# Ones beside the values in the first self-attention, and two preparations moved in program order

## The chip, the cores and the metric

The kernel runs on one core of one Trainium2 chip. The metric is the device time of one execution in microseconds (us). Engines are named PE (TensorE, matrix multiplication), DVE (VectorE), ACT (ScalarE), POOL (GpSimd) and SP (SyncE, which here only issues transfers). Line numbers such as L463 are those of the kernel before.

## The reference

The program is a small two-layer decoder over x of 4 x 256 x 256, with a context ctx_2048 of 4 x 1601 x 256 and a padding mask of 4 x 1601. For the change only the first layer matters: a self attention with 16 heads of 16, then an attention over the context with the mask, then a feed forward whose two weights are made ternary. Cut to the steps concerned:

```python
w = softmax(where(causal, q @ k.T / sqrt(16), -inf))    # 16 heads of 16, per batch
x = x + (w @ v) @ Wo + bo
s = where(mask, NEG, layernorm(x) @ ctx.T)              # 1601 context rows, per batch
x = x + softmax(s) @ ctx
gamma = mean(abs(w))                                    # for w_fc and w_proj, once
w_hat = sign(round(w / (gamma + 1e-6))) * gamma         # ternary weight
```

## The kernel before

The four batches (b = 0 to 3) pass one after another, and overlapping, through four generators: self_attention (L336), memory_attention (L524), feed_forward (L633) and recurrence (L694). A loop of ticks (from L1372) advances each generator by one step per tick; batch b starts at tick START[b] = 0, 3, 9, 15. From some point on a second part takes over, with an attention over the context by pairs of heads and experts, which fills most of the span; the change does not touch it.

The order of instructions on each engine is not written out by hand. The generators emit a program, and a scheduler decides each engine's queue from it. There is one means to hold it: `behind` (L1349) advances a generator and ties every instruction it emits after the latest instruction emitted so far on the same engine. It is used for the first two steps of batches 1 to 3, for the making of the ternary weights and for the first tables of the second part.

self_attention, per batch: layer norm, transposition to features, projection to queries and keys (pq, added to the bias on DVE at L371) and values (pv, L377, added at L381 into a tile v of the batch, 256 values per row), rotation, and norms per head. Then four groups of four heads (c = 0, 1 and e = 0, 1; the names carry batch, c, e, so sc2110 is batch 2, c = 1, e = 1, first half). For each group:

- scores sc: a causal mask is put into the banks with bf16 matmuls (L445), then query times key (L451). Two double banks exist, and one group uses both.
- row maxima mx on DVE (L455, L456), then eight exponentials on ACT (L463), each of which also accumulates its row sum in `sums`;
- the reciprocal of the sums on DVE (L467);
- transposes of the probabilities on PE (tpp L474, tpq L480), copied to SBUF: pT by ACT (L475), tpq's by DVE (L483);
- attention times values on PE (po, L489 and L492), with 32 columns of values at a time, that is two heads of which one is used; copied by ACT (oT, L496), transposed back (tb, L500), and multiplied with the reciprocals on DVE into `a` (L502).

At the end `a` is transposed, multiplied with wo and added to x (L516, L520).

memory_attention, per batch: its first step prepares the mask. A tile mk of bytes is set to zero by DVE, two small transfers on SP's queue fill it, DVE makes from it a float mask mf (L533) and a count cnt (L535), PE transposes mf and sums cnt (xpm, L537 and L538), and DVE copies the results (mb, ok, from L540). mk, mf and cnt have one buffer each. Then come a norm, scores against the transposed context in four pieces (xcT, 512 KB each on SP's queue, xsc L562) with mb as the bias (L565), maxima (xacc, L569 to L573; xtm, xbc), exponentials, and the product with the context (xct, xpo L607). Pieces of the context, and the temporaries `neg` of shared_weights, share the NDB = 3 buffers of one tag.

shared_weights (L303), called tern in the loop: per weight (wfc, wpj: 128 x 2048 each) a sum of magnitudes on DVE (L309), a matmul that adds over partitions (pgg, L311), small operations for the thresholds, then twice a comparison (L323) and a multiplication-like step (L324) of 128 x 1024; at the end a small table hmr (16 KB) is loaded on ACT's queue and two tiles of kron are made. It begins at tick TERN = 20 and goes one step per tick.

Of the kernel before, what the change touches and what calls it, by code (L numbers as in the profile page):

```python
# [20 lines left out]
P = 128  # L21
B, S, D = 4, 256, 256
# [3 lines left out]
NKEY = S + S2  # L26
NCH = 15
NS = 12
H0, HD0 = 16, 16
NKV, REP, HD1 = 4, 4, 128  # L30
# [1 line left out]
NA = 3  # L32
NDB = 3
NROPE = 3
TERN = 20
SIDE = 24
SIDEN = 4
RATE = 1
# [71 lines left out]
def decoder_kernel(ctx: ExitStack, tc: tile.TileContext, at, t, out):  # L110
    nc = tc.nc
    V, A, G, T = nc.vector, nc.scalar, nc.gpsimd, nc.tensor
# [41 lines left out]
    def fa(b, name, dt=F32):  # L154

        return fr.tile([P, 512], dt, tag=f"a{b}", name=name, bufs=NA)
# [9 lines left out]
    def sm(shape, tag, name, bufs=2, dt=F32):  # L166
        return small.tile(shape, dt, tag=tag, name=name, bufs=bufs)

    xs = [const.tile([P, 2, D], F32, tag=f"x{b}", name=f"x{b}") for b in range(B)]

    def load_x(b):
# [47 lines left out]
    def moments(xb, nm):  # L221

        mv = sm([P, 2, 2], "mv", f"mv_{nm}")
        for j in range(2):
            st = sm([P, 6], "bnst", f"st_{nm}{j}")
            V.bn_stats(st, xb[:, j, :])
            V.bn_aggr(mv[:, j, :], st)
        return mv

    def rsqrt(v, eps, nm, n=2):  # L230

# [55 lines left out]
    bqkv, bo, dtb = rows[:, 0:768], rows[:, 768:1024], rows[:, 1024:1280]  # L287
# [48 lines left out]
    def self_attention(b):  # L336
# [25 lines left out]
        for j in range(2):  # L362
            js = slice(j * P, (j + 1) * P)
            pq = p1(f"pq{b}{j}")
            for e in range(2):
                for c in range(2):
                    T.matmul(
                        pq[:, e * 256 : e * 256 + 256], lhsT=xx[:, e, c, js], rhs=wqkv[:, c, e * 256 : e * 256 + 256],
                        start=c == 0, stop=c == 1,
                    )  # L370
            V.tensor_add(qk[:, j, :], pq, bqkv[:, 0:512])  # L371
            yield
        v = fa(b, f"v{b}").rearrange("p (j d) -> p j d", j=2)
        pv = p1(f"pv{b}")
        for j in range(2):
            for c in range(2):
                T.matmul(  # L377
                    pv[:, j * 256 : j * 256 + 256], lhsT=xx[:, 1, c, j * P : (j + 1) * P], rhs=wqkv[:, c, 512:768],
                    start=c == 0, stop=c == 1,
                )  # L380
        V.tensor_add(v, pv.rearrange("p (j d) -> p j d", j=2), bqkv[:, None, 512:768].to_broadcast([P, 2, D]))  # L381

        hd = [P, 2, 32, HD0]
        q4 = qk.rearrange("p j (h d) -> p j h d", d=HD0)
# [4 lines left out]
        rs = cc("r0s").rearrange("p (j d two) -> p j d two", j=2, two=2)  # L389
# [27 lines left out]
        yield  # L417

        if b == 0:
            for e in range(2):  # L420
                V.tensor_scalar(
                    qln[:, e, :], cols[:, 20:22], 1.0 / math.sqrt(HD0), cc("par")[:, e : e + 1], ALU.mult, ALU.mult
                )
        tq = to_features(qkn[:, :, 0:256], f"q{b}")
        qm = fb(b, f"qm{b}").rearrange("p (e n) -> p e n", e=2)
        V.tensor_scalar(qm[:, 0, :], tq, qln[:, 0, 0:1], qln[:, 0, 1:2], ALU.mult, ALU.add)
# [2 lines left out]
        kT = fa(b, f"kT{b}")  # L429
# [4 lines left out]
        for c in range(2):  # L434
            for e in range(2):


                nm = f"{b}{c}{e}"
                mx = sm([P, 2, 4], "mx4", f"mx{nm}", 4)
                sums = sm([P, 2, 4], "sums", f"sum{nm}", 4)  # L440
                scs, es = [], []
                for u in range(2):
                    sc = p2(f"sc{nm}{u}")[0].rearrange("p (h k) -> p h k", h=2)
                    for h in range(2):
                        T.matmul(sc[:, h, 0:384], lhsT=identb, rhs=trib.rearrange("p i k -> p (i k)"), start=True, stop=False)  # L445
                    scs.append(sc)
                q0 = c * 256
                for lo, hi, k0, k1, n in ((0, P, 0, P, P), (P, 2 * P, P, 3 * P, 2 * P)):
                    for i in range(4):
                        r = slice(32 * i, 32 * (i + 1))  # L450
                        T.matmul(  # L451
                            scs[i // 2][:, i % 2, k0:k1], lhsT=qm[r, e, q0 + lo : q0 + hi], rhs=kT[r, c, 0:n], start=False, stop=lo > 0
                        )
                for u in range(2):
                    V.tensor_reduce(mx[:, 0, 2 * u : 2 * u + 2], scs[u][:, :, 0:128], AX.X, ALU.max, negate=True)  # L455
                    V.tensor_reduce(mx[:, 1, 2 * u : 2 * u + 2], scs[u][:, :, 128:384], AX.X, ALU.max, negate=True)  # L456
                yield
                for u in range(2):
                    ex = fb(b, f"sm{nm}{u}").rearrange("p (h k) -> p h k", h=2)
                    for h in range(2):  # L460
                        for j, k in enumerate((slice(0, 128), slice(128, 384))):
                            i = 2 * u + h
                            A.activation(  # L463
                                ex[:, h, k], scs[u][:, h, k], AF.Exp, bias=mx[:, j, i : i + 1], accum_out=sums[:, j, i : i + 1]
                            )
                    es.append(ex)
                V.reciprocal(sums.rearrange("p j h -> p (j h)"), sums.rearrange("p j h -> p (j h)"))  # L467
                yield
                pT = fb(b, f"pT{nm}").rearrange("p (h t) -> p h t", h=4)
                for u in range(2):  # L470
                    tp = p1(f"tpp{nm}{u}")
                    for h in range(2):
                        for j in range(2):
                            T.transpose(tp[:, (2 * h + j) * P : (2 * h + j + 1) * P], es[u][:, h, j * P : (j + 1) * P], ident)  # L474
                    A.copy(pT[:, 2 * u : 2 * u + 2, :].rearrange("p h t -> p (h t)"), tp)  # L475

                tp = p1(f"tpq{nm}")
                for u in range(2):
                    for h in range(2):
                        T.transpose(tp[:, (2 * u + h) * P : (2 * u + h + 1) * P], es[u][:, h, 256:384], ident)  # L480
                for u in range(2):
                    src = tp[:, 2 * u * P : 2 * (u + 1) * P].rearrange("p (h t) -> p h t", h=2)
                    V.tensor_copy(es[u][:, :, 384:512], src)  # L483
                yield

                po = p1(f"po{nm}")
                for i in range(4):
                    f = slice(c * P + 32 * i, c * P + 32 * i + 32)
                    T.matmul(po[32 * i : 32 * i + 32, 0:256], lhsT=v[:, 0, f], rhs=pT[:, i, :], start=True, stop=False)  # L489
                for i in range(4):  # L490
                    f = slice(c * P + 32 * i, c * P + 32 * i + 32)
                    T.matmul(  # L492
                        po[32 * i : 32 * i + 32, 128:256], lhsT=v[:, 1, f], rhs=es[i // 2][:, i % 2, 384:512], start=False, stop=True
                    )
                oT = es[0][:, 0, 0:256]
                A.copy(oT, po[:, 0:256])  # L496
                yield
                tb = p1(f"tb{nm}")
                for j in range(2):
                    T.transpose(tb[:, j * P : (j + 1) * P], oT[:, j * P : (j + 1) * P], ident)  # L500
                for j in range(2):
                    V.tensor_mul(  # L502
                        a[:, j, c * P : (c + 1) * P].rearrange("p (r e d) -> p r e d", e=2, d=16)[:, :, e, :],
                        tb[:, j * P : (j + 1) * P].rearrange("p (r e d) -> p r e d", e=2, d=16)[:, :, e, :],
                        sums[:, j, :, None].to_broadcast([P, 4, 16]),
                    )
                yield
        G.tensor_tensor(xb, xb, bo[:, None, :].to_broadcast([P, 2, D]), ALU.add)
# [15 lines left out]
    def memory_attention(b):  # L524
        xb = xs[b]
        last = S2 - 12 * P

        mk = sm([NC2, P], "mk", f"mk{b}", 1, U8)
        V.memset(mk, 0.0)
        nc.sync.dma_start(out=mk[0:12, :], in_=t["mask"][b, 0 : 12 * P].rearrange("(c p) -> c p", p=P))  # L530
# [9 lines left out]
        V.tensor_copy(mb, pm[:, 0:NC2])  # L540
        ok = sm([P, 1], "ok", f"ok{b}")
        V.tensor_scalar(ok, pm[:, 64:65], 1.0, None, ALU.min)
        mv = moments(xb, f"xa{b}")
        r1 = rsqrt(mv[:, :, 1], 1e-5, f"xa{b}")
        yield
# [7 lines left out]
        for i in range(4):  # L553
            n = 4 if i < 3 else 1
# [793 lines left out]

    def behind(gen, end=None):  # L1349

        ins = nc.cur_bb.bb.instructions
        n = len(ins)
        said = next(gen, end)
        latest = {}
        for i in ins[:n]:
            latest[i.engine] = i
        for i in ins[n:]:
            if i.engine in ENGINES and i.engine in latest:
                tc.add_manual_dep(
                    i, latest[i.engine].name,  # L1360
                    mybir.DependencyInfo(mybir.DependencyClass.NoSync, mybir.DependencyReason.DATA), reason="order",
                )
        return said


# [102 lines left out]
```

## Time and profile before

| what | us |
|---|---|
| median of 3 runs | 1842.06 (1841.42 to 1842.9) |
| the profiled execution | 1839.59 |
| its span | 1837.7, granted clock 0.971 |
| PE busy | 1727.6 (94%) |
| DVE busy | 1288.4 (70%) |
| ACT busy | 1007.2 (55%) |
| POOL busy | 871.8 (47%) |

The profile is of one execution. A group's row has engine, operation and tile, count, busy time, mean duration in ns and the idle time just before its instructions; a row of the timeline has start, duration and, in brackets, the idle time before and what ended it. Granted clock is the share of full speed that PE's throttle allowed. The page's picture of the span in 40 slices of 46 us, cut to four rows, shows PE less busy in the first three or four slices than later:

```profile
PE   4779899989999999999999999999999999999997
DVE  5785647787777677777767786776768676766754
ACT  1556536464656555675656566565746465555631
...
PEclk8789899999999999999999999999999999999998
```

In the chain that ended last, PE has 72% of the span, DVE 10%, ACT 8% and POOL 6%; the largest lines of the chain belong to the second part.

### The profile page before, as it was taken

The numbers are of one execution on the slowest core, as the hardware profiler recorded it, in microseconds if no ns is written. First come the engines' busy times: TensorE is split into PE (matmuls) and PEld (weight loads), VectorE is DVE, ScalarE is ACT, GpSimd is POOL, SyncE is SP. The second block draws the span as 40 slices with busy tenths as digits, with TensorE's granted clock in tenths as the row PEclk, the third lists the DMA queues.
The fourth block names the chain that finished last, engine by engine and source line by source line (L and its number), as shares of the span: only waits on it lengthen the run. The fifth ranks groups of instructions, "written<-read, shape, count | busy, mean of one in ns | idle before, by whom it ended". The sixth has DMA issues, their size and how long they took to land.

```text
span 1837.7 us, 20229 instructions
## 1 busy us (share of the span) xinstructions
PE 1727.6 (94%) x6576; PEld 1051.1 (57%) x6576; DVE 1288.4 (70%) x2396; ACT 1007.2 (55%) x1896; POOL 871.8 (47%) x716
## 2 busy tenths in 40 slices
PE   4779899989999999999999999999999999999997
PEld 3456786655555554645555555656565655656555
DVE  5785647787777677777767786776768676766754
ACT  1556536464656555675656566565746465555631
POOL 2100232111277566566656465555647574555560
PEclk8789899999999999999999999999999999999998
DMA  4010231100210110102010111201111211111110
GB/s 139 1 39 17 73 119 61 32 24 25 67 55 15 52 34 33 38 30 65 17 62 27 63 35 49 61 29 55 34 62 33 68 38 52 32 35 44 32 38 23
DMA packets 66216, 83.00 MB, mean 45 GB/s; under 512 B 6460, under 2 KB 49600, under 8 KB 66112
## 3 DMA queue, kind: packets, MB, share of 16 engines
q1 hardware_dynamic: 64960, 80.31, 14.1%
q10 hardware_dynamic: 1152, 1.41, 0.2%
q8 instruction: 53, 0.87, 0.2%
q14 instruction: 51, 0.42, 0.1%
HBM read 80.65 MB, written 1.05 MB: 44 GB/s over the span
## 4 chain that ended last, share of the span: by engine, by line
PE 72%; DVE 10%; ACT 8%; POOL 6%; issue 4%; POOLq 0%; DVEq 0%; ACTq 0%
PE bsc L1181 18%; PE bpo L1221 17%; PE pk L1115 11%; POOL sum L1212 3%; PE bpw L1247 3%; PE mph L914 2%; PE xpo L607 2%; ACT s L1206 2%; PE xsc L562 2%; ACT s L1182 2%; PE pq L1078 2%; PE mpe L925 1%; ACT sm L463 1%; PE pp L689 1%; PE tpk L1124 1%
## 5 line engine op out<-in xcount | busy, mean ns | idle before, releaser
L1212 POOL TENSOR_TENSOR sum<-sum,s 128x512 f32<-128x512 f32 (+1 forms) x416 | 541.0, 1301 | 81.9 <-ACT s L1206 55.5
L1181 PE MATMUL bsc<-qTb,kTb 128*128 128x512 f32 (+1 forms) x960 | 457.9, 597 | 3.3 <-ACT kTb L1126 3.3
L1221 PE MATMUL bpo<-s,vb 128*128 128x512 f32 (+1 forms) x960 | 456.0, 593 | 0.0
L1182 ACT ACTIVATE s<-bsc,kn 128x512 f32<-128x512 f32 (+1 forms) x480 | 317.8, 685 | 186.1 <-PE bsc L1181 164.4
L1186 DVE SCALAR_TENSOR_TENSOR acc<-bsc,kn,acc 128x512 f32<-128x512 f32 x448 | 333.6, 745 | 110.0 <-ACT s L1182 100.4
L1203 DVE TENSOR_TENSOR s<-s,bc 128x1024 f32<-128x1024 f32 (+1 forms) x256 | 288.4, 1141 | 14.2 <-PE bc L1199 14.0
L1206 ACT ACTIVATE s<-s 128x1024 f32<-128x1024 f32 (+1 forms) x256 | 256.1, 1009 | 60.7 <-DVE s L1203 59.9
L1181 PEld LDWEIGHTS bsc<-qTb,kTb 128*128 128x128 f32 (+1 forms) x960 | 172.1, 187 | 187.8 <-issue 145.8
L1221 PEld LDWEIGHTS bpo<-s,vb 128*128 128x128 f32 (+1 forms) x960 | 173.4, 191 | 141.3 <-issue 136.6
L1040 POOL TENSOR_TENSOR ropek<-ropek,ropuk 128x512 f32<-128x512 f32 (+1 forms) x64 | 76.9, 1201 | 255.9 <-DVE ropuk L1035 255.9
L1115 PE MATMUL pk<-wkv,cTk 128*128 128x256 f32 x832 | 190.1, 379 | 0.0
L1115 PEld LDWEIGHTS pk<-wkv,cTk 128*128 128x128 f32 x832 | 156.7, 190 | 28.4 <-issue 6.2
L1209 POOL TENSOR_TENSOR sum<-s 128x512 f32<-128x512 f32 x32 | 41.8, 1306 | 186.7 <-ACT s L1206 186.7
L1034 DVE TENSOR_TENSOR ropek<-pk,ctabk 128x256 f32<-128x256 f32 (+1 forms) x128 | 51.8, 404 | 70.6 <-ACT squares L1033 69.9
L1033 ACT ACTIVATE squares<-pk 128x256 f32<-128x256 f32 (+1 forms) x128 | 48.1, 377 | 96.3 <-PE pk L1115 74.7
L1047 ACT ACTIVATE ropeq<-ropeq,rnq 128x128 f32<-128x128 f32 x128 | 41.9, 390 | 107.4 <-POOL rnq L1043 107.4
L1184 DVE TENSOR_SCALAR acc<-bsc,kn 128x512 f32<-128x512 f32 x32 | 24.0, 749 | 83.5 <-ACT s L1182 83.5
L1118 ACT COPY vb<-pk 128x256 f32<-128x256 f32 (+1 forms) x128 | 46.3, 362 | 58.7 <-DVE ropuk L1035 56.0
L463 ACT ACTIVATE sm<-sc,mx 128x128 f32<-128x128 f32 (+1 forms) x128 | 52.2, 435 | 26.5 <-DVE mx L456 19.6
L1043 POOL TENSOR_TENSOR kn<-ssk,nhalf 128x4 f32<-128x4 f32 (+1 forms) x64 | 65.5, 1024 | 0.0
L914 PE MATMUL mph<-yTm,wi 128*128 128x256 f32 x256 | 63.2, 392 | 0.0
L1040 POOL TENSOR_TENSOR ropeq<-ropeq,ropuq 128x512 f32<-128x512 f32 x32 | 41.1, 1284 | 40.5 <-DVE ropuq L1035 40.5
(491 smaller groups left out, 2482.8 us busy)
## 6 DMA issues: line engine op xcount, KB each, us to landing
cTk<-in_ctxT SPq DMA_DIRECT2D x32, 512.0 KB, 3.6
wq<-in_wq SPq DMA_DIRECT2D x16, 512.0 KB, 4.9
wo<-in_wo SPq DMA_DIRECT2D x16, 512.0 KB, 4.0
wi<-in_wi SPq DMA_DIRECT2D x32, 256.0 KB, 2.9
xcT<-in_ctxT SPq DMA_DIRECT2D x12, 512.0 KB, 3.7
xct<-in_ctx SPq DMA_DIRECT2D x12, 512.0 KB, 3.7
cTk<-in_ctxT SPq DMA_DIRECT2D x16, 384.0 KB, 3.2
wkv<-in_wkv SPq DMA_DIRECT2D x16, 256.0 KB, 3.8
```

The lines of the kernel that those rows point to most:

```text
L463: A.activation(ex[:, h, k], scs[u][:, h, k], AF.Exp, bias=mx[:, j, i : i + 1], accum_out=sums[:, j, i : i + 1])
L914: T.matmul(ph[:, i * 256 : i * 256 + 256], lhsT=wi[:, i, c, f * ME : (f + 1) * ME], rhs=yT[:, c, :], start=c == 0, stop=c == 1,)
L1040: G.tensor_tensor(r4, r4, u4[:, :, ::-1, :], ALU.add)
L1043: G.tensor_tensor(rn, ss[:, 0:n], nhalf[:, 0:n], ALU.pow)
L1115: T.matmul(pk[:, q, :], lhsT=src, rhs=e["wkv"][:, c, :], start=c == 0, stop=c == 1)
L1181: T.matmul(pc[0:n, :], lhsT=e["kT"][:, k * P : k * P + n], rhs=q, start=True, stop=True)
L1182: A.activation(s[0:n, i, :], pc[0:n, :], AF.Copy, scale=e["kn"][0:n, k : k + 1])
L1186: V.scalar_tensor_tensor(self.acc[0:n, :], pc[0:n, :], e["kn"][0:n, k : k + 1], self.acc[0:n, :], ALU.mult, ALU.max)
L1203: V.tensor_tensor(s[0:n, 0:w, :], s[0:n, 0:w, :], self.bc[0:n, None, :].to_broadcast([n, w, 512]), ALU.subtract)
L1206: A.activation(s[0:n, 0:w, :], s[0:n, 0:w, :], AF.Exp)
L1212: G.tensor_tensor(self.sum[0:n, :], self.sum[0:n, :], s[0:n, i, :], ALU.add)
L1221: T.matmul(self.po, lhsT=e["v"][0:n, k, :], rhs=self.s[c][0:n, i, :], start=k == 0, stop=k == NCH - 1)
```

## The change

Five edits. (1) The values move from a tile of each batch to eight tiles `spots` that lie in buffers otherwise used only later; each head has 32 columns, 16 values and 16 ones, and the ones are set once by POOL at the start. The matmul po then takes the 32 columns of one head, and its columns 16 to 31 give the row sums. The exponentials no longer accumulate sums; the reciprocal is taken from the transposed product tb. (2) The copies of tpq go from DVE to ACT. (3) The addition of the value bias is split in two per batch. (4) `behind` is split into `latest` and `keep_behind`, and these now also tie the mask's preparation of memory_attention and two small operations qln of batch 0 after what was emitted before them. (5) TERN goes from 20 to 36. The core of the diff:

```diff
-TERN = 20
+TERN = 36
+    spots = [ ... ]  # two 128x512 pieces per batch, of tags "v", "kT" and "sum"
+    spots = [w.rearrange("p (h d) -> p h d", d=2 * HD0) for w in spots]
+    for w in spots:
+        G.memset(w[:, :, HD0:], 1.0)
...
+    def keep_behind(before):
+        last, n = before
+        for i in nc.cur_bb.bb.instructions[n:]:
+            if i.engine in ENGINES and i.engine in last:
+                tc.add_manual_dep(i, last[i.engine].name, ... NoSync ..., reason="order")
...
-        v = fa(b, f"v{b}").rearrange("p (j d) -> p j d", j=2)
+        v = spots[2 * b : 2 * b + 2]
...
-        V.tensor_add(v, pv..., bqkv[:, None, 512:768].to_broadcast([P, 2, D]))
+        for j in range(2):
+            V.tensor_add(v[j][:, :, 0:HD0], pv[:, j * 256 : j * 256 + 256]..., bqkv[:, 512:768]...)
...
+            so_far = latest()
             for e in range(2):
                 V.tensor_scalar(qln[:, e, :], cols[:, 20:22], ...)
+            keep_behind(so_far)
...
-                A.activation(ex[:, h, k], scs[u][:, h, k], AF.Exp, bias=mx[...], accum_out=sums[:, j, i : i + 1])
+                A.activation(ex[:, h, k], scs[u][:, h, k], AF.Exp, bias=mx[:, j, i : i + 1])
...
-                V.reciprocal(sums..., sums...)
...
-                    V.tensor_copy(es[u][:, :, 384:512], src)
+                    A.copy(es[u][:, :, 384:512], src)
...
-                    f = slice(c * P + 32 * i, c * P + 32 * i + 32)
-                    T.matmul(po[32 * i : 32 * i + 32, 0:256], lhsT=v[:, 0, f], rhs=pT[:, i, :], ...)
+                    h = 8 * c + 2 * i + e
+                    T.matmul(po[32 * i : 32 * i + 32, 0:256], lhsT=v[0][:, h, :], rhs=pT[:, i, :], ...)
...
+                tb4 = tb[:, 0:256].rearrange("p (j r d) -> p j r d", j=2, r=4)
+                rs = sm([P, 2, 4], "sums", f"sum{nm}", 4)
+                V.reciprocal(rs, tb4[:, :, :, HD0])
                 for j in range(2):
-                    V.tensor_mul(a[...], tb[...], sums[:, j, :, None].to_broadcast([P, 4, 16]))
+                    V.tensor_mul(a[...], tb4[:, j, :, 0:HD0], rs[:, j, :, None].to_broadcast([P, 4, 16]))
...
+        so_far = latest()
         mk = sm([NC2, P], "mk", f"mk{b}", 1, U8)
         ...
         V.tensor_scalar(ok, pm[:, 64:65], 1.0, None, ALU.min)
+        keep_behind(so_far)
```

More of the change, by code (lines that the diff above doesn't have):

```diff
@@ L167, in sm @@
         return small.tile(shape, dt, tag=tag, name=name, bufs=bufs)
+    spots = [
+        w[:, 512 * i : 512 * (i + 1)]
+        for w in (
+            wk.tile([P, NCH * HD1], F32, tag="v", name="values0"), wk.tile([P, NKEY], F32, tag="kT", name="values1")
+        )
+        for i in range(3)
+    ] + [fr.tile([P, 512], F32, tag="sum", name=f"values{i}", bufs=2) for i in (2, 3)]
+    spots = [w.rearrange("p (h d) -> p h d", d=2 * HD0) for w in spots]
+    for w in spots:
+        G.memset(w[:, :, HD0:], 1.0)
     xs = [const.tile([P, 2, D], F32, tag=f"x{b}", name=f"x{b}") for b in range(B)]
@@ L228, in moments, with latest @@
         return mv
+    def latest():
+        ins = nc.cur_bb.bb.instructions
+        return {i.engine: i for i in ins}, len(ins)
+    def keep_behind(before):
+        last, n = before
+        for i in nc.cur_bb.bb.instructions[n:]:
+            if i.engine in ENGINES and i.engine in last:
+                tc.add_manual_dep(
+                    i, last[i.engine].name,
+                    mybir.DependencyInfo(mybir.DependencyClass.NoSync, mybir.DependencyReason.DATA), reason="order",
+                )
     def rsqrt(v, eps, nm, n=2):
@@ L380, in self_attention @@
                 )
-        V.tensor_add(v, pv.rearrange("p (j d) -> p j d", j=2), bqkv[:, None, 512:768].to_broadcast([P, 2, D]))
+        for j in range(2):
+            V.tensor_add(
+                v[j][:, :, 0:HD0], pv[:, j * 256 : j * 256 + 256].rearrange("p (h d) -> p h d", d=HD0),
+                bqkv[:, 512:768].rearrange("p (h d) -> p h d", d=HD0),
+            )
         hd = [P, 2, 32, HD0]
@@ L439, in self_attention @@
                 mx = sm([P, 2, 4], "mx4", f"mx{nm}", 4)
-                sums = sm([P, 2, 4], "sums", f"sum{nm}", 4)
                 scs, es = [], []
@@ L462, in self_attention @@
                             i = 2 * u + h
-                            A.activation(
-                                ex[:, h, k], scs[u][:, h, k], AF.Exp, bias=mx[:, j, i : i + 1], accum_out=sums[:, j, i : i + 1]
-                            )
+                            A.activation(ex[:, h, k], scs[u][:, h, k], AF.Exp, bias=mx[:, j, i : i + 1])
                     es.append(ex)
-                V.reciprocal(sums.rearrange("p j h -> p (j h)"), sums.rearrange("p j h -> p (j h)"))
                 yield
@@ L487, in self_attention @@
                 for i in range(4):
-                    f = slice(c * P + 32 * i, c * P + 32 * i + 32)
-                    T.matmul(po[32 * i : 32 * i + 32, 0:256], lhsT=v[:, 0, f], rhs=pT[:, i, :], start=True, stop=False)
+                    h = 8 * c + 2 * i + e
+                    T.matmul(po[32 * i : 32 * i + 32, 0:256], lhsT=v[0][:, h, :], rhs=pT[:, i, :], start=True, stop=False)
                 for i in range(4):
-                    f = slice(c * P + 32 * i, c * P + 32 * i + 32)
+                    h = 8 * c + 2 * i + e
                     T.matmul(
-                        po[32 * i : 32 * i + 32, 128:256], lhsT=v[:, 1, f], rhs=es[i // 2][:, i % 2, 384:512], start=False, stop=True
+                        po[32 * i : 32 * i + 32, 128:256], lhsT=v[1][:, h, :], rhs=es[i // 2][:, i % 2, 384:512], start=False, stop=True
                     )
@@ L503, in self_attention @@
                         a[:, j, c * P : (c + 1) * P].rearrange("p (r e d) -> p r e d", e=2, d=16)[:, :, e, :],
-                        tb[:, j * P : (j + 1) * P].rearrange("p (r e d) -> p r e d", e=2, d=16)[:, :, e, :],
-                        sums[:, j, :, None].to_broadcast([P, 4, 16]),
+                        tb4[:, j, :, 0:HD0], rs[:, j, :, None].to_broadcast([P, 4, 16]),
                     )
@@ L1349, in behind @@
     def behind(gen, end=None):
-        ins = nc.cur_bb.bb.instructions
-        n = len(ins)
+        before = latest()
         said = next(gen, end)
[L1354 to L1362, printed above, removed]
+        keep_behind(before)
         return said
```

## The prediction, made before the changed kernel was run

> **What bounds the kernel now.** I read five views in this order: busy time by engine in stretches, then the groups of instructions and the timelines of TensorE (PE), VectorE (DVE) and ScalarE (ACT) over the first 260 us. First the stretches, whose columns are the stretch, its length, busy us (instructions) of PE, weight load, DVE, ACT and POOL, then PE's granted clock, DMA share and GB/s:
> ```profile
> 0.00:52.00 52.00, 21.66 (x68) 15.69 (x68) 33.05 (x101) 8.91 (x13) 11.77 (x17) 0.78 0.37 123
> 52.00:95.00 43.00, 35.23 (x246) 23.01 (x247) 32.08 (x80) 25.25 (x87) 8.90 (x9) 0.83 0.00 1
> 95.00:130.00 35.00, 25.85 (x202) 18.02 (x200) 32.78 (x72) 18.61 (x67) 3.41 (x3) 0.80 0.08 24
> 130.00:165.00 35.00, 32.49 (x286) 20.79 (x287) 23.20 (x67) 28.21 (x113) 0.71 (x1) 1.00 0.15 47
> 500.00:1837.00 1337.00, 1304.07 (x4443) 759.04 (x4442) 945.28 (x1530) 750.28 (x1290) 778.70 (x630) 0.99 0.14 42
> ```
> After 500 us PE is busy 97.5% and the change has no instruction there. Everything is decided before, where PE idles 30 us of the first 52, then 7.8, 9.2, 2.5 and (165 to 260) 7.8. Between 95 and 130 the bound is DVE, busy 32.8 of 35. DVE's timeline says with what, PE's what it costs (brackets: idle time ahead, and who ended it):
> ```profile
> 19.11 0.21 DVE L533 TENSOR_SCALAR mf<-mk 13x128 f32<-13x128 uint8 x1 [7.46 <-DMA mk<-in_mask]
> ...
> 98.55 2.28 DVE L309 TENSOR_REDUCE partg<-wfc 128x1 f32<-128x2048 f32 x1
> ...
> 112.81 0.41 DVE L455 TENSOR_REDUCE mx<-sc 128x2 f32<-128x256 f32 x1
> ```
> ```profile
> 83.86 0.60 PE L445 MATMUL sc<-trib,identb 128*128 128x384 bf16 x2 [3.99 <-ACT sm L463]
> ...
> 115.97 0.80 PE L445 MATMUL sc<-trib,identb 128*128 128x384 bf16 x2 [4.14 <-ACT sm L463]
> ...
> 123.26 0.59 PE L311 MATMUL pgg<-partg,cst 128*128 128x1 f32 x2 [3.30 <-DVE partg L309]
> ...
> 214.03 1.28 PE L474 MATMUL tpp<-cst,sm 128*128 128x128 f32 x3 [3.77 <-ACT sm L463]
> 215.29 1.97 PE L562 MATMUL xsc<-hT,xcT 128*65 128x256 f32 x4
> ...
> 247.06 1.03 PE L562 MATMUL xsc<-hT,xcT 128*65 128x256 f32 x4
> ```
> A group's scores wait for the exponentials of the group before (both double banks are taken), those for the row maxima (mx), and these sit in DVE's queue behind copies and ternary weights.
>
> **The mask at the start.** DVE stands 7.46 us for batch 0's mask, which lands 7.3 us after its issue, behind five large loads; the first query-key addition follows at 19.63, though PE had its operand at about 14.2. Gone with the mask kept behind: the next bound is the second half's matmuls, whose last ends at 17.2, where the second addition stood at 21.64. I take 4.2. The two tiny qln operations moved later gain nothing (ACT loads its table then); POOL's eight new memsets (0.2 to 0.7 each by its rows for 128x128 and 128x256, 1.6 to 5 in all) lie in POOL's wait for constants and before the square root wanted at 7.0: 0, at most +2.
>
> **Sums out of the exponentials.** Groups by shape over the first 240 us, then ACT's timeline:
> ```profile
> L463 ACT ACTIVATION_READ_ACCUMULATOR sm<-sc,mx 128x1 f32 x128 | 28.2, 220 | 0.0
> L483 DVE COPY sm<-tpq 128x256 f32<-128x256 f32 x32 | 12.2, 416 | 7.9 <-PE tpq L480 7.8
> L467 DVE RECIPROCAL sum<-sum 128x8 f32<-128x8 f32 x16 | 3.2, 198 | 9.5 <-ACT sm L463 9.4
> ```
> ```profile
> 55.03 0.37 ACT L463 ACTIVATE sm<-sc,mx 128x128 f32<-128x128 f32 x1 [1.89 <-DVE mx L456]
> 55.30 0.19 ACT L463 ACTIVATION_READ_ACCUMULATOR sm<-sc,mx 128x1 f32 x1
> 55.39 0.46 ACT L463 ACTIVATE sm<-sc,mx 128x256 f32<-128x256 f32 x1
> ```
> The 28.2 us of reads overlap: a read delays the next start by 0.09 (55.30 to 55.39). So 128 x 0.09 = 11.5 us leave ACT, and a group of eight exponentials takes 2.6 instead of 3.3. Against that ACT gets the 32 copies of tpq: by its own 128x256 copy (389 ns, 0.28 from start to start) 16 x 0.56 = 9.0. ACT comes out 2.5 shorter. DVE loses 12.2 of copies, the 7.9 it idled in its queue for them and most of the 9.5 before reciprocals. The reciprocal, now from PSUM ahead of the two multiplications, adds 0.2 per group to a step seldom late. Attention times V keeps count and shape of matmuls (32 columns: one head and ones instead of two heads): 0. Four V additions of 128x512 become eight of 128x256: 4 x 0.1.
>
> **Ternary weights later.** Two reductions of 2.28, four comparisons of 0.75, four multiplications of 1.27 (13 us), two kron products of 0.41, two tiny matmuls and a 16 KB load on ACT's queue leave 98 to 143. That removes the 3.30 wait at 123.26 and most of what stands ahead of the maxima at 112.8. By the built program's order they go among batch 2's last groups: weight 0's matmul after that batch's fourth transposes, weight 1's after batch 1's context scores. The temporaries share buffers with context loads: batch 0's three 512 KB loads go early, and batches 1 and 2 now wait for DVE's ternary steps.
>
> **What this gives, walked through.** 52 to 95: exponentials 0.7 shorter and copies (1.3 busy, 0.8 idle) out of DVE's queue bring the maxima about 3 earlier; the 3.99 becomes about 2 and the slow stretch behind it goes: 4.5. 95 to 130: the scores held to 115.97 come where their exponentials allow; what is late next is ACT, with pT, tpq and oT copies in one row, and POOL's square root, so of 9.2 idle and some 4 of half-clock loss I take 9.5. 130 to 165: 1. With the start: 4.2 + 4.5 + 9.5 + 1 = **19** (bounds 10 and 24).
>
> Here the Trainium skill ("TensorE: Matmul & The Clock Gate", "HAM oscillation — how this bites in real kernels") bears: an idle gap of PE over some 3.4 us halves its clock, and in its example each gap costs 1.67 us at that half clock. Rows first: after the 3.77 gap four matmuls take 1.97, against 1.03 at 247.06, and the granted clock is 0.80 in 95 to 130 against 1.00 after it. From PE's busy time and missing clock in three stretches of 20 us I estimate 13.9 x 0.17 + 15.4 x 0.13 + 15.6 x 0.21 = 7.7 us lost between 80 and 140, and about 6 of that is in my 19; by the page's example three gaps would lose 3 x 0.8 = 2.5, and the gain would be 15. I take the rows: here half clock lasts 7 to 10 us after a gap, not 1.7. The rule also speaks against the change, which makes a new long gap (below); but before already pays there, after 3.77, so I charge no second penalty (at worst 3).
>
> **The mask kept behind: what it costs.** For each batch the memset, two small loads on SP's queue, the float mask and count (DVE), transposition and matmul (PE) and two copies now stand where the program has them. PE's queue is in order, so all behind the transposition waits. Batch 0: PE still has 4.6 us of work ahead: 0. Batch 1: 0.6, plus up to 1 for a context load. Batch 3: about 1.4. Batch 2 is the dear one. The built order on DVE ahead of its memset: the attention maxima, two comparisons, wpj, angles, wpj, then small operations. On the clock of the broadcast that ended at 203.7 (t): maxima end t+10.5; 0.67 + 0.67 + 1.2 + 1.1 + 1.2 = 4.85, small ones 2.0: memset t+17.5. The load: nearest row above is a 16 KB load in 1.6 us (hmr), below the first mask's 7.3; behind three 512 KB loads I take 3.0, so the float mask at t+20.5. PE reaches the transposition at t+7.6: it idles 12.7 instead of 3.77, and behind it stand the probabilities' transposes, batch 1's maximum, and batch 2's first context scores. The maximum's transposes slip from t+15.9 to t+23.4: 7.5. Sum of losses: 0.6 + 0.5 + 1.4 + 7.5 = **10**. The skill speaks against this move too ("DMA: Bandwidth & Descriptors", "Rules for kernel authors"): issue a load early and wait for it late, so that its fixed cost is covered. Before's rows agree for masks 1 to 3, which cost no stall; now 3.0 of load stands in the chain of batches 2 and 3 and partly of batch 1. With the loads left early I would write 10 - 2 x 3.0 - 0.5 = 3.5 of loss.
>
> **Sum.** Against the profiled execution (span 1837.7, itself 1839.6): -19 + 10 = -9, so 1830.6. That execution lies 2.5 below the median of 1842.1, so I put the median at **1833**.
>
> **Rivals.** *The waits are covered* (0.18): DVE reaches the third memset earlier because all upstream came forward, or batch 2's slip is taken up by later idle time; the loss shrinks to 0 to 3: 1823 to 1826. For it: PE has 7.8 of idle in 165 to 260 to absorb; against: order within a queue. *The gain is given back to ACT* (0.15): tpq's copies, formerly beside ACT's own, are in the chain probabilities, copy, attention; all 16 x 0.56 = 9 exposed leave 10 of the gain, the loss is 10: 1842, no change. For it: ACT is 81% busy in 130 to 165; against: reads shrink by more. *Slower* (0.12): mask loads just before their use queue behind the 512 KB context loads and take the 7.3 of the first mask instead of 3.0. Masks 1, 2 and 3 stand in front of PE, so each us counts thrice: loss 10 + 3 x 4.3 = 23 against 19, 1846. It decides once a load takes over 3.0 + (9 + 3.7)/3 = 7.2. For it: in SP's queue mask 2 follows three such loads; against: 3.7 us each, issued earlier.
>
> **Numbers.** Main case 0.55 (1826 to 1838). A measurement tells 0.2% (3.7 us, so 1838.4 to 1845.7) from no change. Main gives 0.52 faster, 0.03 same; covered 0.18 faster; ACT 0.13 same, 0.02 slower; slower 0.09 slower, 0.03 same: 0.70, 0.19, 0.11. Range 1820 to 1844: from a gain of 24 to the ACT case.
>
> **What would show it.** No mask wait on DVE before 20 us; no accumulator reads, tpq's copies on ACT with 0.28 a step; the gaps of 3.99, 4.14 and 3.30 gone and clock near 1.0 in 95 to 130; the probability transposes of batch 3's fourth group behind a PE wait of about 12 us at batch 2's mask; after 500 us PE unchanged. Wrong if that gap is under 5 or over 20, if ACT ends most waits in 52 to 165, or if the upstream gain at batch 0's first broadcast is under 10.

## The result, and the profile after

| | before | after |
|---|---|---|
| median of 7 runs each, us | 1840.97 (1838.07 to 1842.9) | 1834.01 (1833.59 to 1836.38) |
| profiled execution, us | 1839.59 | 1833.72 |
| its span, us | 1837.7 | 1831.9 |

The ratio is 0.9968 with a 95% interval of 0.9956 to 0.9979, so the changed kernel is faster by 0.2 to 0.4%: some 6 us by the ratio, 7 between the two medians. The forecast was 1833.

First the stretches of the kernel after, with the columns of the prediction's first view:

```profile
0.00:52.00 52.00, 24.82 (x89) 17.82 (x89) 36.43 (x105) 10.52 (x17) 15.16 (x26) 0.79 0.45 154
52.00:95.00 43.00, 35.70 (x255) 23.84 (x256) 30.74 (x75) 25.58 (x66) 11.18 (x10) 0.86 0.00 1
95.00:130.00 35.00, 31.80 (x271) 20.46 (x272) 22.38 (x60) 26.05 (x72) 0.00 (x0) 0.95 0.08 24
130.00:165.00 35.00, 32.73 (x274) 21.80 (x273) 20.18 (x61) 25.09 (x70) 1.41 (x2) 1.00 0.00 1
165.00:260.00 95.00, 78.53 (x428) 63.98 (x427) 54.91 (x112) 39.57 (x86) 24.67 (x15) 0.91 0.27 82
```

DVE is no longer the bound of 95 to 130 (22.4 busy instead of 32.8), PE has 271 matmuls there instead of 202, and its granted clock is 0.95 instead of 0.80. But in 165 to 260 PE is idle for 16.5 instead of 7.8. The row of before:

```profile
165.00:260.00 95.00, 87.16 (x478) 68.83 (x477) 48.55 (x120) 44.01 (x120) 20.87 (x14) 0.91 0.25 75
```

PE's timeline after the change says where:

```profile
78.62 0.80 PE L477 MATMUL sc<-trib,identb 128*128 128x384 bf16 x2 [3.42 <-ACT sm L495]
...
109.83 0.48 PE L477 MATMUL sc<-trib,identb 128*128 128x384 bf16 x2 [1.24 <-ACT sm L495]
...
199.68 1.97 PE L595 MATMUL xsc<-hT,xcT 128*65 128x256 f32 x4 [4.68 <-ACT sm L495]
209.01 0.28 PE L569 MATMUL xpm<-cst,mf 13*128 13x13 f32 x1 [7.35 <-DVE mf L565]
...
248.92 0.23 PE L569 MATMUL xpm<-cst,mf 13*128 13x13 f32 x1 [0.89 <-DVE mf L565]
```

The wait of 4.14 is down to 1.24, that of 3.30 is gone, that of 3.99 is still 3.42, and at batch 2's mask PE now stands 4.68 + 7.35 = 12.0 us, where it stood 3.77. DVE's timeline shows the start and, from 198 us on, what stands ahead of that mask:

```profile
15.04 0.69 DVE L398 TENSOR_TENSOR qk<-pq,rows 128x512 f32<-128x512 f32 x1 [3.42 <-PE pq L394]
...
17.53 0.69 DVE L398 TENSOR_TENSOR qk<-pq,rows 128x512 f32<-128x512 f32 x1 [0.39 <-PE pq L394]
...
198.41 0.68 DVE L488 TENSOR_REDUCE mx<-sc 128x2 f32<-128x512 f32 x1
199.01 1.40 DVE L350 TENSOR_SCALAR negg<-wpj,log 128x1024 f32<-128x1024 f32 x2
200.33 1.27 DVE L351 SCALAR_TENSOR_TENSOR wpj<-wpj,hig,negg 128x1024 f32<-128x1024 f32 x1
201.53 1.14 DVE L1015 SCALAR_TENSOR_TENSOR ang<-sn,ang 128x960 f32<-128x960 f32 x1
202.60 1.27 DVE L351 SCALAR_TENSOR_TENSOR wpj<-wpj,hig,negg 128x1024 f32<-128x1024 f32 x1
...
206.90 0.09 DVE L561 MEMSET mk<- 13x32 uint32 x1
208.68 0.27 DVE L565 TENSOR_SCALAR mf<-mk 13x128 f32<-13x128 uint8 x1 [1.69 <-DMA mk<-in_mask]
```

The query-key additions start when PE delivers, not when a mask lands. After the last maxima come two ternary comparisons (negg), wpj, angles, wpj, small operations, and only then the memset; the float mask mf waits 1.69 more for the load.

To follow the time through the kernels I use four points of PE's timeline: the first transposed queries (tp_q), the broadcasts of batch 0's and batch 1's memory attention (xbc), and a mark near 480 us, the start of the recurrence's last output projection (spw). From the mark on, the distance between two kernels stays the same within 0.6 us until about 1740 us (in loads_early within 1.8). Up to it all kernels do the same 2092 matmuls, so that a difference in PE's busy time there is chiefly one of clock, and the rest is idle time; the stretches up to the mark, of before and then of after:

```profile
0.00:485.90 485.90, 409.42 (x2092) 285.05 (x2092) 332.59 (x851) 247.49 (x589) 89.77 (x83) 0.91 0.18 55
```
```profile
0.00:479.22 479.22, 403.84 (x2092) 280.24 (x2092) 323.65 (x823) 245.09 (x493) 92.85 (x91) 0.93 0.18 56
```

Of the 6.7 us gained at the mark, PE's idle time gives only 1.1 (76.5 to 75.4); the same matmuls took 5.6 less, at a granted clock of 0.93 instead of 0.91. The trace also records when the clock changes: before the mark it was at half (0.50) for 85.3 us in the kernel before and for 71.7 after the change. The idle time removed early came back at batch 2's mask; what stayed is the clock.

### The profile page after: what moved, and what is told of

Same layout as the page of the kernel before. It is cut to its first block, busy times and chain, and to the rows that moved or that the text cites. A ratio compares the mean times of both kernels' runs of the same rounds, so it can differ in the third digit from the quotient of the medians.

```text
span 1831.9 us, 20116 instructions
## 1 busy us (share of the span) xinstructions
PE 1721.9 (94%) x6576; PEld 1046.2 (57%) x6576; DVE 1279.4 (70%) x2368; ACT 1005.1 (55%) x1800; POOL 874.1 (48%) x724
## 4 chain that ended last, share of the span: by engine, by line
PE 71%; DVE 11%; ACT 7%; POOL 6%; issue 4%; DMA 1%; ACTq 0%; POOLq 0%; DVEq 0%
PE bsc L1214 18%; PE bpo L1254 17%; PE pk L1148 11%; POOL sum L1245 3%; PE bpw L1280 3%; PE mph L947 2%; ACT s L1239 2%; ACT s L1215 2%; PE pq L1111 2%; PE xsc L595 1%; PE xpo L640 1%; PE mpe L958 1%; PE tpk L1157 1%; ACT ropeq L1080 1%; DVE s L1236 1%
## 5 line engine op out<-in xcount | busy, mean ns | idle before, releaser
L1111 PE MATMUL pq<-wq,yTb 128*128 128x512 f32 x128 | 60.3, 593 | 0.0
```

Source lines behind the costliest of these rows:

```text
L1111: T.matmul(pq, lhsT=d["yT"][:, c, j * P : (j + 1) * P], rhs=e["wq"][:, c, :], start=c == 0, stop=c == 1)
```

## The experiments

Each kernel was timed together with the kernel before, whose median was 1840.97, 1840.89, 1840.73 and 1839.63 in the four sets of rounds; so ratios, not medians, compare kernels of different sets (the last set is mask0_only, copy_only, tern36_only and m0t32). Columns: start of three of the points in us, PE's busy and idle time up to the mark, the mark, span of the profiled execution, median, and ratio to the kernel before with its interval.

| kernel | tp_q | batch 0 xbc | batch 1 xbc | busy | idle | mark | span | median | ratio |
|---|---|---|---|---|---|---|---|---|---|
| before | 48.61 | 203.48 | 220.82 | 409.4 | 76.5 | 485.90 | 1837.7 | 1840.97 | |
| after | 44.65 | 188.24 | 213.78 | 403.8 | 75.4 | 479.22 | 1831.9 | 1834.01 | 0.9968 [0.9956, 0.9979] |
| mask0_only | 44.18 | 199.13 | 216.21 | 407.1 | 74.4 | 481.44 | 1833.5 | 1832.85 | 0.9963 [0.9950, 0.9977] |
| copy_only | 49.03 | 203.09 | 220.45 | 407.7 | 75.5 | 483.16 | 1835.0 | 1836.34 | 0.9981 [0.9972, 0.9989] |
| ones_only | 48.56 | 202.44 | 220.86 | 403.8 | 81.7 | 485.48 | 1840.9 | 1844.18 | 1.0021 [1.0014, 1.0027] |
| tern36_only | 48.55 | 204.25 | 224.47 | 411.3 | 75.9 | 487.23 | 1838.9 | 1843.16 | 1.0014 [1.0006, 1.0022] |
| accum | 44.15 | 194.96 | 220.57 | 403.2 | 82.3 | 485.45 | 1840.8 | 1842.71 | 1.0016 [1.0008, 1.0023] |
| dvecopy | 44.48 | 196.44 | 222.28 | 410.5 | 78.8 | 489.29 | 1841.9 | 1845.73 | 1.0023 [1.0014, 1.0031] |
| tern20 | 44.31 | 190.44 | 214.19 | 403.8 | 75.4 | 479.21 | 1834.6 | 1839.18 | 0.9991 [0.9983, 0.9999] |
| mask0 | 44.27 | 189.02 | 211.41 | 409.3 | 69.2 | 478.51 | 1831.1 | 1831.86 | 0.9949 [0.9935, 0.9963] |
| loads_early | 48.02 | 194.20 | 213.71 | 410.0 | 76.7 | 486.66 | 1839.9 | 1842.31 | 1.0008 [0.9999, 1.0016] |
| loads_early2 | 44.27 | 190.33 | 215.07 | 402.4 | 77.7 | 480.16 | 1832.7 | 1838.17 | 0.9990 [0.9982, 0.9998] |
| m0t28 | 44.20 | 197.38 | 214.35 | 407.8 | 68.1 | 475.89 | 1831.1 | 1834.26 | 0.9968 [0.9957, 0.9979] |
| m0t32 | 44.39 | 192.88 | 209.61 | 404.2 | 69.2 | 473.39 | 1826.0 | 1830.13 | 0.9948 [0.9936, 0.9961] |

A mark says where time went, but it is of one execution, and how far it moves between executions of one kernel is not known. The times of tern20 run from 1836.37 to 1843.07; its profile is of the fastest execution, as are those of m0t32, loads_early2 and dvecopy, and mask0's is of its slowest. So a difference of one to three us at a mark is no proof, and the ratios decide whether a kernel is faster. Each edit also lets the scheduler order the queues anew, so a difference is that of the edit with its order.

**The masks of batches 1 to 3 free (mask0).**

```diff
-        so_far = latest()
+        so_far = latest() if b == 0 else ({}, 0)
```

> The changed kernel, with the mask's preparation tied behind for batch 0 only. Theory: what the change loses is batch 2's transposition of the mask, where PE stands 4.7 + 7.35 us. Free again, it leaves the chain batch 1 maximum, which still has two ternary steps of the second weight ahead on DVE: its transposes come at about 207.1 in place of 212.5, so 5.4 less: 1828.5. Rival (the long wait is taken up by later idle time): 1834, as the changed kernel. Rival (the ternary steps alone hold it): 1832 or more.

The median is 2.2 below the changed kernel's, where 5.4 were expected; batch 1's broadcast comes only 2.4 earlier, and the mark 0.7. PE's timeline shows why:

```profile
199.47 2.71 PE L503 MATMUL tpp<-cst,sm 128*128 128x128 f32 x8 [3.67 <-ACT sm L495]
206.88 0.66 PE L610 MATMUL xtm<-cst,xacc 128*128 128x128 f32 x2 [1.88 <-DVE rse_xa L260]
211.41 0.66 PE L615 MATMUL xbc<-cst,xmq 128*128 128x128 f32 x2 [3.87 <-DVE nmr L288]
```

The wait at the mask is gone. The maximum's transposes (xtm) came at 206.9, as expected (207.1); the wait of 3.87 behind them was not expected. DVE's timeline names it:

```profile
209.07 1.86 DVE L356 TENSOR_TENSOR kron<-hmr,cst 128x256 f32<-128x256 f32 x2 [1.94 <-DMA hmr<-in_hmrep]
210.85 0.41 DVE L612 TENSOR_REDUCE xmq<-xtm 128x2 f32<-128x256 f32 x1
```

The ternary comparisons stand where they stood. But the two kron products, which come at 216.75 in the changed kernel, behind batch 1's broadcast, now stand ahead of its maximum (xmq), and DVE waits 1.94 for their small table hmr and then works 1.86 on them. So a new stall took the place of a part of the old one.

PE's idle time up to the mark is still 6.1 less than in the changed kernel (69.2 against 75.4). The mark is only 0.7 earlier because PE's busy time is 5.4 more: the clock is at half for 81.9 us instead of 71.7, in part long ahead of this mask (17.1 us instead of 10.2 between 77 and 119). By the ratios mask0 is the better of the two, though the intervals still touch.

**The mask loads early (loads_early, loads_early2).** Four buffers of mk, memset and loads ahead of the tie:

```diff
-        so_far = latest()
-        mk = sm([NC2, P], "mk", f"mk{b}", 1, U8)
+        mk = sm([NC2, P], "mk", f"mk{b}", 4, U8)
...
+        so_far = latest()
         mf = sm([NC2, P], "mf", f"mf{b}", 1)
```

> The changed kernel, with the memset and the two loads of each mask free to go early (four buffers), and only the float mask and what follows tied behind. Theory: the load is 1.7 of the wait at batch 2's mask (1.69 idle ahead of the float mask), the DVE list is the rest: 1832. Rival of the prediction (the load is 3.0 of it, and counts for batches 2 and 3): 1828. Rival (no part of the wait shows at the end): 1834.

This missed, by its own making: the instruction last emitted on DVE is now the memset itself, so the float mask is tied only behind that. Batch 0's float mask went to the front again, and DVE's wait with it:

```profile
19.25 0.21 DVE L565 TENSOR_SCALAR mf<-mk 13x128 f32<-13x128 uint8 x1 [7.71 <-DMA mk<-in_mask]
```

Inside the changed kernel this costs 3.4 us at tp_q and 7.4 at the mark, of which 1.3 are idle time and 6.1 busy time (half clock for 85.3 us instead of 71.7). It is not the price of that wait alone, since the later masks are no longer held on DVE either: at batch 2's mask PE waits for nothing (its float mask is made at 174.4), the kron products stay behind (216.71), and batch 1's broadcast follows batch 0's by 19.5, in the changed kernel by 25.5.

In loads_early2 the tie is taken ahead of the memset and applied from the float mask on:

```diff
         so_far = latest()
-        mk = sm([NC2, P], "mk", f"mk{b}", 1, U8)
+        mk = sm([NC2, P], "mk", f"mk{b}", 4, U8)
...
+        so_far = so_far[0], latest()[1]
         mf = sm([NC2, P], "mf", f"mf{b}", 1)
```

> The changed kernel with the memsets and mask loads at the start (four buffers), and the float mask and all that follows tied behind what the changed kernel ties them to. Theory: the load is 1.7 of the wait at batch 2's mask, DVE's list the rest; no stall at the start, since the float mask stays behind: 1832. Rival (a step earlier on DVE lets something else come later, nothing at the end): 1834. Rival of the prediction (3.0 a load, for two batches): 1828.

Batch 2's wait is 6.56 instead of 7.35, batch 1's broadcast follows batch 0's by 24.7 instead of 25.5, and the mark is 0.9 later than in the changed kernel. The float mask starts earlier, as expected: 18.6 after the start of batch 0's broadcast instead of 20.4. But it takes 1.27 instead of 0.27 and ends at 210.24, just after an operation of POOL (208.77 to 210.17); whether the one held the other was not tried. So with 1.8 of load and memset out of the way only 0.8 of wait is won, and nothing at the mark: the prediction's 3.0 a load is too high. By its ratio this kernel is slower than the changed one, the intervals apart; the profiled execution, its fastest (span 1832.7), does not show where; that stays open.

**The ternary weights at the old tick (tern20), and moved alone (tern36_only).** The one edit is TERN = 20 in the changed kernel, TERN = 36 in the kernel before.

> The changed kernel with the ternary weights at the old tick. Theory: in 95 to 165 DVE gets 13 us back and the upstream gain shrinks by about 6; at batch 2's mask 3.6 of DVE's list are gone, so the wait is that much shorter: 1836.5. Rival (the upstream gain came from the exponentials and copies, the ternary weights had cover): 1830. Rival (the ternary weights were most of it): 1840.

> The kernel before with the ternary weights begun at tick 36 alone. Theory: the wait of 3.3 for the weights' matmul and DVE's backlog ahead of the maxima go, 3 to 5 at batch 0's broadcast, and 2 to 4 come back where the ternary steps stand ahead of batch 1's maximum: 1840. Rival (the prediction: most of 9.5 in 95 to 130 is theirs): 1834.

In the changed kernel the old tick costs 2.2 at batch 0's broadcast and nothing at the mark (479.21 and 479.22); alone, the new tick makes the mark 1.3 later, and batch 1's broadcast comes 20.2 after batch 0's instead of 17.3. Both expectations were too high on the early gain. In the profiled executions the move is worth nothing at the mark, in busy time or idle time. By the ratios it is worth some 4 us in the changed kernel (0.9968 against 0.9991, the intervals apart) and costs 0.1% alone. 2.7 of tern20's loss is the end of the run, by its profile; the rest is open.

**tpq's copies (dvecopy, copy_only).** `A.copy` against `V.tensor_copy`, in the changed kernel and in the one before.

> The changed kernel with tpq's copies on DVE again. Theory: with the ternary weights gone DVE has room in 95 to 165, so the copies cost only where they stand ahead of the maxima (0.76 each and some idle time): about +3, 1837. Rival (the copies in DVE's queue were what held the maxima): +8, 1842. Rival (ACT is the bound after the change, the copies are better on DVE): 1831.

> The kernel before with tpq's copies on ACT and nothing else. Theory: with the row sums still read, ACT holds 9 more in the groups and DVE 12 less; taking reads out alone gave nothing at the end, putting the copies back cost 10: the two parts work only together, so 1839 to 1843, ACT ending the waits of PE. Rival (the copies alone carry the gain): 1834.

Back on DVE they cost 10.1 at the mark (3.5 idle, 6.6 busy, with half clock for 92.2 us), 8.2 of it at batch 0's broadcast: more than the theory's 3, and nearest to the first rival's 8. Alone they give 2.7 at the mark and 0.2% by the ratio, where the theory had expected no gain and its rival 5 or more.

**The row sums (ones_only, accum).** ones_only is the changed kernel with the copies on DVE, no ties and TERN = 20. accum puts the sums back where nobody reads them:

```diff
-    A.activation(ex[:, h, k], scs[u][:, h, k], AF.Exp, bias=mx[:, j, i : i + 1])
+    A.activation(ex[:, h, k], scs[u][:, h, k], AF.Exp, bias=mx[:, j, i : i + 1], accum_out=old[:, j, i : i + 1])
```

> The kernel before with the ones beside the values, the split addition and the moved reciprocal alone (tpq's copies on DVE, mask and ternary weights as before). Theory: a group's exponentials are 0.7 shorter and the reciprocals no longer stand in DVE's queue waiting for them, but the maxima still sit behind copies and ternary weights: about 3 less than before, 1838. Rival (the sums were what held the queues): 1834 or less. Rival (the read's time on ACT was idle time anyway): 1841.

> The changed kernel, with the exponentials accumulating their row sums again into a tile that nothing reads: the price of 128 reads on ACT by themselves. Theory: ACT is in the chain of each group, some 5 of the 16 groups wait for it on PE, 0.7 each: 1834 + 3.5 = 1837.5. Rival (all 128 x 0.09 show): 1845. Rival (none): 1834.

Alone the ones give 0.4 at the mark, but by the ratio that kernel is slower than before, by 0.1 to 0.3%: all three expectations missed. In the profile 3.6 of it is the end, from the mark on (1355.4 against 1351.8). With the copies on ACT, the reads cost 6.2 at the mark, nearly twice what I expected. Up to the mark PE is idle 82.3 us with them and 75.4 without, so the cost is waiting and not clock, and PE's timeline names ACT:

```profile
163.21 3.72 PE L596 MATMUL xsc<-hT,xcT 128*128 128x256 f32 x16 [2.61 <-ACT sm L496]
171.14 3.72 PE L596 MATMUL xsc<-hT,xcT 128*128 128x256 f32 x16 [1.21 <-ACT sm L496]
```

**The first mask alone (mask0_only).** The kernel before, with batch 0's preparation tied behind.

> The kernel before with the mask's preparation of batch 0 alone tied behind. Theory: the wait at the start is worth 4 at batch 0's first transposed queries (48.6 to 44.6), as in the changed kernel; since the later waits are unchanged, 3 to 4 of it are left: 1837. Rival (the gain is met by the wait for the maxima and lost): 1841.

4.4 at tp_q, 4.35 at batch 0's broadcast, 4.5 at the mark: nothing of it is lost on the way. By its ratio (0.9963) this single tie does what the whole change does (0.9968).

**Free masks and another tick (m0t28, m0t32).** mask0 with TERN = 28 and 32.

> The changed kernel with the mask tied behind for batch 0 only, and the ternary weights begun at tick 28 (their last step then stands ahead of batch 3's last group on DVE). Theory: batch 1's broadcast was late after the change because the ternary steps of the second weight and the mask's wait stood in one chain; with both away it follows batch 0's by 17.3 as in the kernel before (25.5 in the changed one, 22.4 with the mask free alone), 5 less than with the mask free alone, and up to 2 is lost earlier: 1828. Rival (the chain is then set by ACT and POOL, not by DVE's list): 1832, as with the mask free alone.

> The changed kernel with the mask tied behind for batch 0 only, and the ternary weights begun at tick 32, between the two placings tried. Theory: between the 478.5 and 475.9 that these reached at the last common point near 480 us (479.2 in the changed kernel), so 3 less than the changed kernel there, and at the end 1829 to 1833, as the clock in the last 40 us falls. Rival (each placing only moves the wait): 1834 to 1836.

In m0t32 batch 1's broadcast follows batch 0's by 16.7, less than before (17.3), and 10.6 of the early gain of 15.2 is kept:

```profile
199.27 0.17 PE L569 MATMUL xpm<-cst,mf 13*128 13x13 f32 x1
...
203.33 1.09 PE L503 MATMUL tpp<-cst,sm 128*128 128x128 f32 x3 [3.67 <-ACT sm L495]
...
208.58 0.42 PE L610 MATMUL xtm<-cst,xacc 128*128 128x128 f32 x2 [0.37 <-DVE xacc L606]
209.61 0.40 PE L615 MATMUL xbc<-cst,xmq 128*128 128x128 f32 x2 [0.61 <-DVE xmq L612]
```

Its mark is 5.8 earlier than the changed kernel's, more than expected (3), and its ratio (0.9948) is the lowest of all, but level with that of mask0 (0.9949). PE's idle time up to the mark is the same in both (69.2); the 5.1 between their marks is busy time, with the clock at half for 64.9 us instead of 81.9. m0t28 has 68.1 idle, and by its ratio it is level with the changed kernel, where the theory had expected 6 us less. So what shows in all three kernels with free masks is 6 to 7 us less idle time; a better tick for the ternary weights is not shown.

## Why the prediction came out right, step by step

- **The start.** 4.2 forecast; 3.96 at tp_q, and 4.4 with that edit alone. Shown.
- **Exponentials and copies.** A group of eight takes 2.6, as forecast (last of the views below), and up to the mark ACT's busy time falls by 2.4 (2.5 forecast). DVE's falls by 8.9. Views: the maxima ahead of the wait of 3.99, before and after, and the exponentials behind them, after.

```profile
80.85 0.42 DVE L455 TENSOR_REDUCE mx<-sc 128x2 f32<-128x256 f32 x1
```
```profile
75.98 0.42 DVE L487 TENSOR_REDUCE mx<-sc 128x2 f32<-128x256 f32 x1
```
```profile
77.22 2.60 ACT L495 ACTIVATE sm<-sc,mx 128x128 f32<-128x128 f32 x8 [1.65 <-DVE nr_hf L270]
```

- **52 to 95: the step that was mis-sized.** "The maxima about 3 earlier" is wrong: they start at 75.98 instead of 80.85, and 3.96 of these 4.87 are the start's. So the copies' removal moved them by 0.9. Ahead of them DVE still has the next batch's norms, and the scores themselves end only at about 75.2. The wait of 3.99 became 3.42, not 2, and the slow stretch behind it did not go: the clock is at half for 6.83 us in both kernels. Batch 2's transposed queries (89.93 to 84.90) give 1.1 for this stretch instead of 4.5.
- **95 to 165.** 10.5 forecast. Batch 0's output projection moves from 152.66 to 139.12, 13.54 in all and 8.5 since batch 2's queries. Up to batch 0's broadcast another 1.7 came. Upstream sum: 15.2 instead of 19.

```profile
152.66 1.99 PE L516 MATMUL pw<-wo,aT 128*128 128x256 f32 x8
```
```profile
139.12 1.89 PE L547 MATMUL pw<-wo,aT 128*128 128x256 f32 x8
```

- **Batch 2's mask.** Idle 12.0 against 12.7; memset at t+18.4 against 17.5; load 1.69 against 3.0, beside the lower row of 1.6; slip of batch 1's broadcast 8.2 against 7.5. The size was right, and the mask is the larger part of it. Batch 1's broadcast follows batch 0's by 25.5 with the mask held and the ternary steps there; by 23.8 with the ternary steps gone and the mask held (tern20); by 22.4 (mask0) or 19.5 (loads_early) with the mask not held; by 16.7 with both away (m0t32). The 22.4 has the stall for hmr in it, the 19.5 has not. So of the 8.8 in all the held mask alone accounts for some 6, the ternary steps alone for 1.8.
- **All losses after batch 0's broadcast** to the mark: 15.2 - 6.7 = 8.5, against 10. Batch 3's mask costs 0.89 idle (1.4 forecast). No second penalty of the clock was charged for the long wait, and none came: PE was busy at half clock for 9.0 us behind the wait of 3.77 before, and for 6.8 around the two waits of 12.0 after.
- **The sum.** 6.7 at the mark and 5.8 at the end of the profiled execution, against 9. The upstream gain was 3.8 too high and the losses 1.5 too high, so part of the nearness is luck: errors of opposite sign. That the median came within 1.0 of 1833 is luck too, since the forecast started from a median of 1842.1 and the later one was 1840.97.
- **The clock.** I put some 6 of the gain, between 80 and 140, on the half clock. There the record shows half clock for 6.83 and 13.65 us before (PE busy in 14.9 of them) and for 6.83 and 3.41 after (busy in 8.3). A matmul at half clock takes about twice its time, as the 1.97 against 1.03 of the prediction's lines shows, so I estimate that half of these busy times was lost: 7.5 before, as the prediction had it (7.7), but still 4.2 after. The gain there is 3.3, not 6, nearer to the estimate of 2.5 that the prediction made from the Trainium skill's example ("TensorE: Matmul & The Clock Gate", "HAM oscillation — how this bites in real kernels"), though half clock lasted longer behind each gap than the example's 1.67. The 5.6 of busy time gained up to the mark comes in part from later stretches; that it equals the 6 is chance.
- **A sign that did not tell.** The prediction called itself wrong if ACT ended most of PE's waits in 52 to 165. It does: 11.8 of 13.4 us. But it did so before, too, 17.0 of 20.7, since PE waits there for ACT's exponentials (sm), and these for the maxima; so the sign could not tell the two cases apart.
- **The rivals.** Slower: the load took 1.69, far from 7.2, and loads_early2 gave no gain from moving it. Given back to ACT: not in the change, where the reads left ACT, but accum shows it at once (mark 485.45, before 485.90). Covered: mask0 gains only 0.7 at the mark, but not because later idle time took the wait up: 6.1 of idle time went and 5.4 of busy time came, with more half clock.

How the parts add up is the result that I had not foreseen. Alone they give 4.5 (mask of batch 0), 2.7 (copies), 0.4 (ones) and -1.3 (ternary weights), 6.3 together, against 6.7 for the whole; the ties of the other masks had no run of their own. The ratios agree less well: from them I estimate 6.8 + 3.5 - 3.9 - 2.6 = 3.8 us for the four and 5.9 for the whole. And at batch 0's broadcast the four alone give 4.35 + 0.4 + 1.0 - 0.8 = 5.0, and the whole 15.2. Ones and copies need each other: put back into the whole, the reads cost 6.2 and the copies on DVE 10.1. Why the early 10 between 5.0 and 15.2 appear only together I have not shown beyond the waits named; the queues are ordered anew in each kernel.

## What to carry to other kernels

Follow a gain along the same instructions of both traces, not only to the end: here 15 us were won by the first broadcast and 8.5 were lost right after. Count the same matmuls up to a common point and part their time into busy and idle: in mask0 6.1 us of waiting went, and the clock took 5.4 of it back, which no list of waits shows. When a wait is taken away, look what the scheduler put in its place: in mask0 a stall of 3.8 us for a small table. Tie only the instruction that stalls: batch 0's mask behind was worth 4.5 and cost nothing, while the same tie on the other masks makes PE idle 6 us more.

## What the runs showed of the hardware that was not expected

In all fourteen traces the granted clock is recorded as either 1.0 or 0.5, and it changes only on a grid of 3.41 us: half clock lasts 3.41, 6.83, 10.24, 13.65, 17.07 or 20.48 us (a last stretch that the end cuts off apart). The grid stands differently against the kernel in each execution. Half clock also comes with waits shorter than the 3.4 us of the rule that the prediction cites: near 440 us PE waits 2.44 in every trace, and a stretch of half clock begins between 0.4 us before and 1.4 us after the wait's end.

Near the end all kernels have the same wait, 3.15 to 3.20 us, yet the twelve matmuls soon after it take 2.86 in one execution and 5.21 in another, here the changed kernel and tern20:

```profile
1785.22 1.11 PE L1265 MATMUL ts<-cst,sum 128*128 128x128 f32 x4 [3.15 <-POOL sum L1245]
...
1789.34 2.86 PE L1280 MATMUL bpw<-wo,aT 128*128 128x256 f32 x12 [0.85 <-DVE aT L1273]
```
```profile
1784.91 1.11 PE L1265 MATMUL ts<-cst,sum 128*128 128x128 f32 x4 [3.15 <-POOL sum L1245]
...
1789.43 5.21 PE L1280 MATMUL bpw<-wo,aT 128*128 128x256 f32 x12 [0.85 <-DVE aT L1273]
```

In every trace the clock halves within this wait. In ten it does so 0.22 to 0.70 us before the wait's end, and half clock lasts 3.41; in the other four (ones_only, accum, tern20, m0t28) 0.83 to 1.23 before its end, and half clock lasts 10.24. These four take 1355.2 to 1355.4 us from the mark to the end, the ten 1351.7 to 1353.2, whatever was changed before. So one and the same wait costs some 3 us more, half of what the change gives, according to where it falls on the grid. No run moved the wait on the grid, so this is read from fourteen executions and not tried.
